# A shared expert's second products over all 128 rows of TensorE, with zeros in the matrix, in place of two products of 64 rows

## The chip, the cores and the metric

The kernel runs on one core of a Trainium2 chip. The metric is the time of one execution on the device, in microseconds. Before the change three runs took 928.37, 928.45 and 928.70 us; the median is 928.45.

## The reference

Eight sequences of 512 tokens with 128 features pass through three steps, each with a residual: an expert layer (weight 0.5), a mixing layer, and the same expert layer again. All matrices are float32. The expert layer has 64 routed experts and one shared expert, each with 64 hidden features. What it computes on a normalized token matrix `xf`:

```
shared = silu(xf @ Ws_up) @ Ws_down                     # (T,128)->(T,64)->(T,128)
cw     = weights of the 8 best of 64 experts per token, else 0
h      = silu(einsum('td,edf->etf', xf, W_up))          # all 64 experts
y      = einsum('etf,efd->etd', h, W_down)
out    = shared + einsum('etd,te->td', y, cw)
```

The change concerns the last product of `shared`, with `Ws_down` of 64 x 128.

## The kernel before

**Items and pairs.** An item is one sequence in one of the two expert layers, so there are 16 items of 512 tokens. Data is held transposed: features on the partitions, tokens along the free axis. Experts are taken two at a time, as two experts of 64 hidden features fill the 128 rows: 32 pairs for each item. For pair n, `up(n)` multiplies by `W_up` (`up_part`, L527) into an accumulator `ph` in PSUM and takes the silu on ScalarE into a tile `h` (L538). `scale(n)` multiplies `h` by the routing weights `cw` on VectorE (L544), which come by DMA from a scratch tensor. `down(n)` multiplies by `W_down` and adds into the item's accumulator `ys[i]`, 128 x 512 (L554).

**Order.** The order is written out by hand: one loop over n = 0 ... 32 x 16 + 14 does `up(n)`, the scaling of a pair some 20 steps back, and `down(n - 25)`. Engines work through their instructions in the order in which the program gives them, and on TensorE `up` and `down` products alternate. Between them generators insert the preparation of the next item (`prep`: normalization, the product for the router and the shared expert at L393, selection of experts), the mixing layer (L292, L299) and the residual (`finish`).

**The shared expert.** `prep(i)` computes the shared expert's hidden features, silu at L436, for one item at a time, 64 rows. Even items write rows 0 to 63 of a tile `hsh`; the following odd item writes rows 64 to 127 of the same tile. So `shared[i]` and `shared[i+1]` are one tile with two sequences in it.

**The place of the change.** When an even item i reaches pair 12 in `down` (`SHARED`), the accumulator of item i+1 is taken as well, and both items' second products are issued one behind the other at L567. The matrix tile `wsdn` holds `Ws_down` twice, in rows 0 to 63 and in rows 64 to 127. Item i's product takes the lower 64 rows of matrix and hidden tile and adds into `ys[i]`; item i+1's takes the upper 64 and starts `ys[i+1]`. The next products on TensorE are the ordinary `up` and `down` ones.

**Loading.** `wsdn` is loaded by two DMAs from `load_rest` (L160) on SP's queue, behind the first transfers of routing weights and ahead of the second half of `W_down`. On POOL the program begins with an identity matrix, a small constant and one memset of zeros into a part of `cent` (L139).

Of the kernel before, what the change touches and what calls it, by code (L numbers as in the profile page):

```python
# [8 lines left out]
F32 = mybir.dt.float32  # L9
# [4 lines left out]
P = 128  # L14
# [29 lines left out]
def macaron_kernel(  # L44
# [36 lines left out]
    nc = tc.nc  # L81
    B, T, D = x.shape
    E, _, F = w_up.shape
# [7 lines left out]
    const = ctx.enter_context(tc.tile_pool(name="const", bufs=1))  # L91
# [21 lines left out]
    def load_x(s, a=0, e=NT, queue=nc.sync):  # L113
        src = x[s].rearrange("(n p) d -> p n d", p=P)
        queue.dma_start(out=xs[s][:, a:e, :], in_=src[:, a:e, :])
# [2 lines left out]
    wdn = const.tile([P, NP, D], F32, name="wdn")  # L118

    wsl = const.tile([P, 2, 2, F], F32, name="wsl")  # L120
    wsdn = const.tile([P, D], F32, name="wsdn")
    cent = const.tile([P, D], F32, name="cent")
    bias_bc = const.tile([P, E], F32, name="bias_bc")
    wmix = const.tile([D, 2, D], F32, name="wmix")
# [8 lines left out]
    def load_down(e0, e1):  # L133
        nc.sync.dma_start(
            out=wdn[:, e0 // 2 : e1 // 2, :],
            in_=w_down[e0:e1].rearrange("(q two) f d -> (two f) q d", two=2),
        )

    nc.gpsimd.memset(cent[E:, :], 0.0)  # L139

    for n, (a, e) in enumerate(PIECES):
        load_x(0, a, e, (nc.sync, nc.scalar)[n % 2])
# [14 lines left out]
    def load_rest():  # L157

        for k in range(2):
            nc.sync.dma_start(out=wsdn[k * F : (k + 1) * F, :], in_=ws_down)  # L160
        load_down(E // 2, E)
        load_x(2)
        yield
        nc.sync.dma_start(out=wmix[:, 0, :], in_=wb)
        nc.sync.dma_start(out=wmix[:, 1, :], in_=wbf)
        yield
        nc.sync.dma_start(out=w12[:, 0, :], in_=w1[0].partition_broadcast(P))
        nc.sync.dma_start(out=w12[:, 1, :], in_=w2[0].partition_broadcast(P))
        nc.sync.dma_start(out=b_bc, in_=b.partition_broadcast(P))
        for s in range(3, B):  # L170
            yield
            load_x(s)
# [168 lines left out]
    shared = {}  # L341
# [159 lines left out]
    def finish(i, y, last=True):  # L501

        _, s = items[i]
        yield
        yt = norm.tile([P, NT, D], F32, tag="yt", name=f"yt{i}")
        y = y.rearrange("d (n p) -> d n p", p=P)
        yield from blocks(
            lambda f, q: yt[quad(q), :, quad(f)],
            lambda f, q: y[quad(f), :, quad(q)],
            D // B32,  # L510
            P // B32,
        )
        nc.vector.scalar_tensor_tensor(xs[s], yt, 0.5, xs[s], ALU.mult, ALU.add)
        if last:
            store(i, slice(0, NT))
# [34 lines left out]
    def down(n):  # L550
        i, pair = divmod(n, NP)
        if pair == 0 and i not in ys:
            ys[i] = ps_y.tile([P, T], F32, tag="y", name=f"y{i}")
        nc.tensor.matmul(  # L554
            ys[i],
            lhsT=wdn[:, pair, :],
            rhs=hs.pop(n),
            start=pair == 0 and i % 2 == 0,
            stop=pair == NP - 1 or n == total - ENDING - 1,
        )  # L560


        if i % 2 == 0 and pair == SHARED:
            ys[i + 1] = ps_y.tile([P, T], F32, tag="y", name=f"y{i + 1}")
            for k in range(2):
                rows = slice(k * F, (k + 1) * F)
                nc.tensor.matmul(  # L567
                    ys[i + k],
                    lhsT=wsdn[rows, :],
                    rhs=shared[i + k][rows, :],  # L570
                    start=k == 1,
                    stop=False,
                )
        if pair == NP - 1 and i + 1 < len(items):
            finishing.append(finish(i, ys.pop(i)))
# [33 lines left out]
    for n in range(total + DOWN_LAG - ENDING):  # L609
        i, pair = divmod(n, NP)  # L610
        if n < total:
            if i == 0 and pair == FIRST:
                run(coming)
                for g in range(CW_BUFS):
                    load_cw(g)
                loading = load_rest()
                next(loading)
            if i > 0 and pair == 0:
                while i not in shared:
                    next(coming)  # L620
            if i > 0 and pair == LAST_PREP:
                run(coming)
                coming = iter(())
            if i + 1 < len(items) and pair == FIRST_PREP[items[i + 1][0]]:
                coming = prep(i + 1)
            up(n)
# [5 lines left out]
        if n >= DOWN_LAG:  # L632
            down(n - DOWN_LAG)
            if finishing and next(finishing[0], finishing) is finishing:
                finishing.pop(0)
# [51 lines left out]
```

## Time and profile before

| | |
|---|---|
| median of three runs | 928.45 us |
| profiled execution | 928.27 us |
| its span, first to last instruction | 926.5 us |
| granted TensorE clock | 1.00 |
| matmul records at L527 / L554 / L567 | 1040 / 1004 / 32 |
| mean length of a record at L527, 512 columns | 593 ns |
| mean length of a record at L554 | 592 ns |
| mean length of a record at L567 | 641 ns |
| mean length of a weight load at L554 / L567 | 190 / 184 ns |
| DMA, mean rate over the span | 157 GB/s |

A float32 product is carried out in two passes, so it gives two matmul records and two weight loads. The records of matmuls overlap: a record of 592 ns says when a pass began and when its last result was written, and the next pass begins before that. How much of TensorE's time a pass takes is read from the distance between two starts. The profile calls TensorE's matmuls PE and its weight loads PEld; DVE is VectorE, ACT is ScalarE, POOL is GpSimd and SP issues DMAs. L567 means line 567 of the kernel. In a row of the timeline the columns are start and length in microseconds, engine, line, operation, tiles written and read, shapes, the number of instructions merged into the row, and in brackets the engine's idle time before it with what ended it.

### The profile page before, as it was taken

The numbers are of one execution on the slowest core, as the hardware profiler recorded it, in microseconds if no ns is written. First come the engines' busy times: TensorE is split into PE (matmuls) and PEld (weight loads), VectorE is DVE, ScalarE is ACT, GpSimd is POOL, SyncE is SP. The second block draws the span as 40 slices with busy tenths as digits, with TensorE's granted clock in tenths as the row PEclk, the third lists the DMA queues.
The fourth block names the chain that finished last, engine by engine and source line by source line (L and its number), as shares of the span: only waits on it lengthen the run. The fifth ranks groups of instructions, "written<-read, shape, count | busy, mean of one in ns | idle before, by whom it ended". The sixth has DMA issues, their size and how long they took to land.

```text
span 926.5 us, 8543 instructions
## 1 busy us (share of the span) xinstructions
PE 922.6 (100%) x2343; PEld 423.3 (46%) x2343; DVE 749.5 (81%) x2160; ACT 364.2 (39%) x600; POOL 39.8 (4%) x65
## 2 busy tenths in 40 slices
PE   9999999999999999999999999999999999999998
PEld 6444444444444444444444444444444444444445
DVE  6758978849497585969989899898998989989656
ACT  6533434334343343433434334343343433434330
POOL 1000000000000000000000000000000000000000
PEclk9999999999999999999999999999999999999999
DMA  7999986865949578566676756667576675766973
GB/s 179 228 202 204 215 183 143 187 135 134 192 110 193 112 159 164 139 140 135 143 160 138 161 133 157 156 150 164 130 163 151 151 162 128 160 156 151 190 150 84
DMA packets 88704, 145.72 MB, mean 157 GB/s; under 512 B 9616, under 2 KB 21584, under 8 KB 88656
## 3 DMA queue, kind: packets, MB, share of 16 engines
q1 hardware_dynamic: 88288, 145.05, 71.8%
q8 instruction: 18, 0.29, 0.2%
q14 instruction: 30, 0.25, 0.1%
q10 hardware_dynamic: 368, 0.13, 0.1%
HBM read 140.97 MB, written 4.19 MB: 157 GB/s over the span
## 4 chain that ended last, share of the span: by engine, by line
PE 100%; DVE 0%; issue 0%
PE ph L527 48%; PE y L554 47%; PE sl L393 2%; PE y L588 1%; PE y L567 1%; PE pfb L299 1%; PE pfb L292 1%; PE busy L181 0%; PE ps_ft L420 0%; DVE x L595 0%; PE cent_ps L187 0%; DVE zeros L176 0%
## 5 line engine op out<-in xcount | busy, mean ns | idle before, releaser
L527 PE MATMUL ph<-ut,wup 128*128 128x512 f32 (+2 forms) x1040 | 520.3, 586 | 0.0
L554 PE MATMUL y<-h,wdn 128*128 128x512 f32 x1004 | 510.2, 592 | 0.0
L538 ACT ACTIVATE h<-ph 128x512 f32<-128x512 f32 x512 | 300.5, 598 | 465.3 <-PE ph L527 455.0
L544 DVE TENSOR_TENSOR h<-h,cw 128x512 f32<-128x512 f32 x512 | 338.4, 686 | 36.0 <-DMA cw<-cw_t 29.7
L527 PEld LDWEIGHTS ph<-ut,wup 128*128 128x128 f32 x1040 | 194.7, 190 | 237.4 <-issue 231.8
L554 PEld LDWEIGHTS y<-h,wdn 128*128 128x128 f32 x1004 | 190.8, 190 | 240.1 <-issue 200.9
L248 DVE STREAM_TRANSPOSE yt<-y 32x128 f32<-32x128 f32 x256 | 79.9, 312 | 68.3 <-PE y L554 64.2
L248 DVE STREAM_TRANSPOSE ut<-u_f 32x128 f32<-32x128 f32 x240 | 72.2, 301 | 3.6
L248 DVE STREAM_TRANSPOSE aff<-sl 32x128 f32<-32x128 f32 x128 | 40.0, 312 | 4.1 <-PE sl L393 2.0
L248 DVE STREAM_TRANSPOSE mixt<-u_mix 32x128 f32<-32x128 f32 x128 | 38.7, 302 | 2.1
L248 DVE STREAM_TRANSPOSE cw_sb<-cwtok 32x128 f32<-32x128 f32 x128 | 38.4, 300 | 1.8
L228 DVE TENSOR_SCALAR u_f<-x,mv_f,rstd_f 128x128 f32<-128x128 f32 x64 | 18.0, 342 | 19.6 <-POOL rstd_f L224 19.6
L223 POOL TENSOR_SCALAR rstd_f<-mv_f 128x4 f32<-128x4 f32 x15 | 8.3, 552 | 502.9 <-DVE mv_f L222 502.9
L456 ACT ACT_TABLE_LOAD x15 | 19.2, 1283 | 23.4 <-DVE aff L248 23.4
L308 DVE SCALAR_TENSOR_TENSOR pfb<-u_mix,ident,pfb 128x129 f32<-128x129 f32 x16 | 5.7, 356 | 19.6 <-PE pfb L299 19.4
L538 ACT ACT_TABLE_LOAD x16 | 20.5, 1283 | 0.3
L224 POOL TENSOR_TENSOR rstd_f<-rstd_f,minus_half 128x4 f32<-128x4 f32 (+2 forms) x18 | 17.4, 966 | 4.1 <-DVE rstd_f L223 2.8
L228 DVE TENSOR_SCALAR u_mix<-x,mv_mix,rstd_mix 128x128 f32<-128x128 f32 x32 | 8.9, 343 | 9.9 <-POOL mixt L279 9.9
L393 PE MATMUL sl<-ut,wsl 128*128 128x512 f32 (+2 forms) x36 | 16.9, 550 | 0.0
L223 POOL TENSOR_SCALAR rstd_mix<-mv_mix 128x4 f32<-128x4 f32 x8 | 4.6, 576 | 280.0 <-DVE mv_mix L222 280.0
L436 ACT ACTIVATE hsh<-sl 64x512 f32<-64x512 f32 x16 | 9.5, 591 | 16.8 <-PE sl L393 16.8
L219 DVE BATCH_NORM_STATS2 st_f<-x 128x6 f32<-128x128 f32 x64 | 14.0, 277 | 1.9 <-DMA x<-in_L_attn_u_dram 1.8
(61 smaller groups left out, 247.8 us busy)
## 6 DMA issues: line engine op xcount, KB each, us to landing
cw<-cw_t SPq DMA_DIRECT2D x254, 512.0 KB, 6.7
cw_t<-cw_sb SPq DMA_DIRECT2D x16, 128.0 KB, 3.8
x<-in_L_attn_u_dram SPq DMA_DIRECT2D x7, 256.0 KB, 15.4
out_dram<-x SPq DMA_DIRECT2D x7, 256.0 KB, 3.1
wdn<-in_L_ffn_W_down_dram SPq DMA_DIRECT2D x2, 512.0 KB, 5.9
cw<-cw_t SPq DMA_DIRECT2D x4, 256.0 KB, 5.8
wup<-in_L_ffn_W_up_dram SPq DMA_DIRECT2D x4, 128.0 KB, 3.2
wup<-in_L_ffn_W_up_dram SPq DMA_DIRECT2D x1, 512.0 KB, 5.2
```

The source lines that it names most:

```text
L219: nc.vector.bn_stats(st[:, j, :], src[:, j, :])
L223: adds.tensor_scalar(rstd[:, a:e], mv[:, a:e, 1], EPS_LN, None, ALU.add)
L224: nc.gpsimd.tensor_tensor(rstd[:, a:e], rstd[:, a:e], minus_half[:, a:e], ALU.pow)
L228: nc.vector.tensor_scalar(u[:, j, :D], src[:, j, :], mv[:, j, 0:1], rstd[:, j : j + 1], ALU.subtract, ALU.mult,)
L248: nc.vector.transpose(dst(i, q), src(i, q))
L393: nc.tensor.matmul(sl[:, cols], lhsT=wsl[:, odd, :, :].rearrange("d a f -> d (a f)"), rhs=ut[:, cols], start=True, stop=True,)
L436: nc.scalar.activation(hsh[mine, :], sl[mine, :], AF.Silu)
L456: nc.scalar.activation(sig, aff, AF.Sigmoid)
L527: nc.tensor.matmul(ph[:, cols], lhsT=w, rhs=uts[i][:, cols], start=True, stop=True)
L538: nc.scalar.activation(h, ph, AF.Silu)
L544: nc.vector.tensor_tensor(h, h, cw_tiles[group][:, g, :], ALU.mult)
L554: nc.tensor.matmul(ys[i], lhsT=wdn[:, pair, :], rhs=hs.pop(n), start=pair == 0 and i % 2 == 0, stop=pair == NP - 1 or n == total - ENDING - 1,
```

## The change

The matrix tile becomes twice as wide, 128 x 2 x 128. Its first half holds `Ws_down` in rows 0 to 63 and zeros in rows 64 to 127; its second half holds zeros in rows 0 to 63 and `Ws_down` in rows 64 to 127. The zeros are written once, by two memsets on POOL. Both products then take all 128 rows of the matrix and all 128 rows of the hidden tile; the zeros cancel the other sequence's rows. Accumulators, start and stop flags, and the place in the order stay.

```diff
-    wsdn = const.tile([P, D], F32, name="wsdn")
+
+    wsdn = const.tile([P, 2, D], F32, name="wsdn")
...
     nc.gpsimd.memset(cent[E:, :], 0.0)
+    for k in range(2):
+        nc.gpsimd.memset(wsdn[(1 - k) * F : (2 - k) * F, k, :], 0.0)
...
         for k in range(2):
-            nc.sync.dma_start(out=wsdn[k * F : (k + 1) * F, :], in_=ws_down)
+            nc.sync.dma_start(out=wsdn[k * F : (k + 1) * F, k, :], in_=ws_down)
...
         if i % 2 == 0 and pair == SHARED:
             ys[i + 1] = ps_y.tile([P, T], F32, tag="y", name=f"y{i + 1}")
             for k in range(2):
-                rows = slice(k * F, (k + 1) * F)
                 nc.tensor.matmul(
                     ys[i + k],
-                    lhsT=wsdn[rows, :],
-                    rhs=shared[i + k][rows, :],
+                    lhsT=wsdn[:, k, :],
+                    rhs=shared[i + k],
                     start=k == 1,
                     stop=False,
                 )
```

## The prediction

> **What bounds the kernel.** I read the profile in this order: the busy shares, the chain of waits that ended last, the list of waits, and then the timeline of the one place that the change touches. The first three settle what the time is made of.
>
> ```profile
> PE 922.6 (100%) x2343; PEld 423.3 (46%) x2343; DVE 749.5 (81%) x2160; ACT 364.2 (39%) x600; POOL 39.8 (4%) x65
> ...
> PE 100%; DVE 0%; issue 0%
> PE ph L527 48%; PE y L554 47%; PE sl L393 2%; PE y L588 1%; PE y L567 1%; PE pfb L299 1%; PE pfb L292 1%; PE busy L181 0%; PE ps_ft L420 0%; DVE x L595 0%; PE cent_ps L187 0%; DVE zeros L176 0%
> ```
>
> The chain is TensorE from end to end. A busy TensorE alone would prove little, since its matmuls overlap, so the list of waits is needed too. Restricted to matmuls it has a single row:
>
> ```profile
> PE busy L181 <- DVE zeros L176: 1.0, 1, 1.0
> ```
>
> That is the first microsecond of the program. After it no matmul waits for another engine or for a transfer. What a stage costs is then the distance from one matmul's start to the next one's, and whatever is added to it is added to the end. Nothing later takes it back, since there is no later wait of TensorE to shorten.
>
> A product of float32 appears as two matmul records (two passes). Far from the change, passes start every 0.429 us: the last long stretch of the chain in order of time has 32 passes in 13.73 us.
>
> ```profile
> 900.96 13.73 PE y L554 x32
> ```
>
> **The place itself.** The changed products stand at L567, reached eight times (items 0, 2, ... 14), each time two products of two passes: 8 x 2 x 2 = 32 records. The timeline of TensorE around the first of them (start, length, engine, line, count):
>
> ```profile
> 50.73 1.02 PE L554 MATMUL y<-h,wdn 128*128 128x512 f32 x2
> 51.69 1.13 PE L567 MATMUL y<-hsh,wsdn 64*128 64x512 f32 x4
> 52.75 1.12 PE L527 MATMUL ph<-ut,wup 128*128 128x512 f32 x2
> 53.71 1.02 PE L554 MATMUL y<-h,wdn 128*128 128x512 f32 x2
> 54.57 1.02 PE L527 MATMUL ph<-ut,wup 128*128 128x512 f32 x2
> ```
>
> The reader is to look at the starts. The ordinary distance between two pairs of passes is 54.57 - 53.71 = 0.86 us. The four passes of L567 take 52.75 - 51.69 = 1.06 us where four at the ordinary rate take 1.72. So the two halves of the array do work at once: in the trace's starts, two passes begin within 0.01 us of each other, and the next two 0.53 us later. But the overlap isn't free. The pair before L567 occupies 51.69 - 50.73 = 0.96 us instead of 0.86, the pair after it again 53.71 - 52.75 = 0.96. The row of weight loads says why:
>
> ```profile
> 51.69 0.30 PEld L567 LDWEIGHTS y<-hsh,wsdn 64*128 64x128 f32 x4 [0.76 <-issue]
> ```
>
> Ordinary loads follow the previous one after an idle 0.24 us, while the pass before is still running. These start only after 0.76 us, together with their own passes: at the boundary the weights are not loaded ahead, and the array runs empty for about 0.10 us going in, and again coming out. The list of waits has that row eight times, 6.1 us in all, so 0.76 at every place.
>
> **The sum, part by part.** From 50.73 to 53.71 there are eight passes (two of L554, four of L567, two of L527) and they take 2.98 us. After the change all eight use all 128 rows. There are as many instructions as before, but none can share the array with another, so they run one after another with their weights loaded ahead: 8 x 0.429 = 3.43 us. The difference is 3.43 - 2.98 = +0.45 us (0.46 with the starts to the nanosecond), split so: four passes that lose their partner, 1.72 - 1.06 = +0.66; the two boundaries that go, 2 x 0.10 = -0.20. The stretch around the last of the eight places has the same starts (854.91, 855.86, 856.92, 857.88: 2.97 us), so I multiply by eight: **+3.65 us**, all of it on the path.
>
> _A rule against the trace._ The row: two passes on different halves start together, but each place costs 2.98 us in all. The Trainium skill, "TensorE: Matmul & The Clock Gate", Part 3, "Measured speedup vs the span model", says a group of tiles lasts as long as one matmul plus about 4 ns for each further tile. By that alone the present products would cost two passes of 0.429 at each place, and separating them would add 2 x 0.429 = 0.86 us, eight times 6.9 us. The trace agrees with the rule on the near-simultaneous starts, but the rule leaves out the slower starts around and inside the group, 4 x 0.10 us at each place. I take the row: +3.65, not +6.9. Both speak against this change; neither the rule nor the row offers a way to profit from it except the boundaries, and these are too small.
>
> **The other edits.** _Two memsets on POOL_, of 64x128 each. The nearest row is the one for `cent`, of the same size, and the row after it is what could be delayed:
>
> ```profile
> 1.41 0.20 POOL L139 MEMSET cent<- 64x128 f32 x1
> ...
> 3.68 1.10 POOL L224 TENSOR_TENSOR rstd_f<-rstd_f,minus_half 128x1 f32<-128x1 f32 x2 [2.08 <-DVE rstd_f L223]
> ```
>
> They are 2 x 0.20 = 0.40 us, put directly behind `cent` and ahead of POOL's first useful work, the power at L224, which waits 2.08 us for VectorE anyway. Cost nothing; without this cover they would delay the first normalization by up to 0.4 us. No DMA is issued from POOL there, and the issues of SP and ScalarE are not behind them. _The two loads of the matrix_ (SP, L160) keep size and count; the rows land at another stride. Issued at 28.4 and 29.5, landed at most 16.0 us later, so by 45.5, while the first use is at 51.69: 6.2 us to spare.
>
> _Waits that are added._ Each product now reads all 128 rows of the hidden tile, so item i's product needs item i+1's half too, and both need the zeros. Behind a waiting product stands everything on TensorE, its queue being the kernel's bound. But the second product needed that half already, and it is written long before:
>
> ```profile
> 34.63 0.59 ACT L436 ACTIVATE hsh<-sl 64x512 f32<-64x512 f32 x1 [1.12 <-PE sl L393]
> ```
>
> 35.2 against 51.69; at the last place 842.8 against 855.86. The zeros are set near 2 us. What handling further wait conditions costs TensorE itself is not in the trace as a row of its own. From below: nothing, as for the products of L554, which also wait for another engine's semaphore and still start every 0.43 us. From above: a pause like the ones at L567, 0.10 us at each place, 0.8 in all. A gain is excluded, since a wait can't start anything earlier. I take nothing, the nearer row.
>
> _Work behind._ VectorE, ScalarE and the DMA queue get 0.45 us more time per place. Their waits fall a little; none of them is on the chain.
>
> **Sum.** The profiled execution took 928.27 us, of which 926.5 are its span and 1.8 lie around it; with +3.65 it is 931.9. The median of the runs is 0.18 higher, 928.45, so I predict **932.1**.
>
> **Rivals.** _The pauses stay_ (10%). If the 0.10 us at the four starts came from something else than the 64-row form, such as the fresh accumulator of item i+1 or the switch between two operand sets, the eight full passes would keep them and cost 3.43 + 0.40 = 3.83 us: +0.85 a place, +6.8 in all, 935.3. Against it: ordinary products alternate accumulator, weights and operand at every pair and show no pause. In part, with one pause left at each place, it gives 932.9.
>
> _A new wait decides_ (3%). If the matrix landed over 6.2 us later than now, TensorE would stand at the first place; only there, since the matrix is loaded once. A landing twice as late (32 us) would give 61.5 - 51.7 = 9.8 us, 942. Against it: the same bytes in the same order.
>
> _Not slower_ (5%). The one mechanism: full-row passes without a mode change hand over faster than I assume, because two following products stream the same hidden tile. To come out even, the four passes would have to take 1.72 - 0.45 = 1.27 us, 0.32 each; only then is the removal of the boundaries worth what the sharing was. At 0.32, the time is 928.5. Against it: no pass of 512 columns in the trace starts less than about 0.43 us after another on the same rows, whatever it reads.
>
> _It doesn't do what it says_: if the present two products had not overlapped, the change would only remove pauses. The 1.06 us for four passes exclude that.
>
> **How the numbers follow.** The likeliest case has 82%, with a range of its own from 931.7 to 932.9 (rounding of the starts and scatter of the runs below; one pause left at each place above). The range on record, 931.2 to 933.4, adds part of the first rival; its full form and the other two stay outside. A difference of 0.2%, 1.9 us, is about what a measurement of this kernel can tell from no change. The likeliest case and the first two rivals are slower by more than that; the third divides between no change (3%) and faster (2%).
>
> **What would show it.** In the changed profile: L567 as 32 records of 128*128, starting 0.43 us apart; no 0.76 us of idle before their weight loads, 0.24 instead; the stretch from L554's first pass to the next L554 3.43 us at all eight places; TensorE still with no wait after the first microsecond, and span and TensorE's busy time both longer by 3.6 to 3.7 us. Pauses that remain, a stop at the first place, or starts closer than 0.43 us would make the prediction wrong.

## The result and the profile after

The changed kernel took 932.61 us (median of four runs, 932.24 to 933.18) against 928.55 before. The ratio is 1.0040 with a 95% interval of 1.0028 to 1.0051: slower, with the whole interval above 1. The time lies inside the range, 0.5 us above the forecast. The profiled execution is the slowest of the four, 933.18, with a span of 931.4.

The timeline of TensorE around the first place, after the change (line numbers from L530 to L568 stand for L527 to L567 before):

```profile
50.59 1.02 PE L557 MATMUL y<-h,wdn 128*128 128x512 f32 x2
51.45 1.88 PE L568 MATMUL y<-hsh,wsdn 128*128 128x512 f32 x4
53.17 1.02 PE L530 MATMUL ph<-ut,wup 128*128 128x512 f32 x2
54.03 1.02 PE L557 MATMUL y<-h,wdn 128*128 128x512 f32 x2
```

The four passes take 53.17 - 51.45 = 1.72 us, and the distances ahead of them and behind are 0.86 each. From L557 to L557 it is 3.44 us where it was 2.98. In the starts to the nanosecond every one of the eight places shows the same: six passes from the second of L557 to the second of L530 in 2.575 us, where it was 2.115. That is +0.46 each and +3.68 in all, so the forecast's term is there in full. The weight loads show the same: each follows after the ordinary idle time of 0.24 us instead of 0.76.

```profile
51.02 0.19 PEld L568 LDWEIGHTS y<-hsh,wsdn 128*128 128x128 f32 x1 [0.24 <-issue]
51.45 0.19 PEld L568 LDWEIGHTS y<-hsh,wsdn 128*128 128x128 f32 x1 [0.24 <-issue]
```

But the span grew by 4.9, not by 3.7. The page and the waits of TensorE's matmuls show the rest:

```profile
PE 926.2 (99%) x2343; PEld 427.2 (46%) x2343; DVE 749.6 (80%) x2160; ACT 364.0 (39%) x600; POOL 40.1 (4%) x67
...
PE 96%; DVE 2%; ACT 0%; issue 0%; DMA 0%; POOL 0%; ACTq 0%; POOLq 0%
```

```profile
PE busy L184 <- DVE zeros L179: 1.0, 1, 1.0
PE ph L530 <- ACT h L541: 1.0, 1, 1.0
```

TensorE's busy time grew by 926.2 - 922.6 = 3.6 us, as it should, but there is one wait more, and 4% of the chain runs through other engines. That is no 4% of lost time: for some 25 us the chain follows VectorE and ScalarE while TensorE still works, and only the wait at its end is lost. The timeline has this stop of TensorE near 103 us, TensorE first, then ScalarE:

```profile
102.95 1.02 PE L557 MATMUL y<-h,wdn 128*128 128x512 f32 x2
104.99 1.13 PE L530 MATMUL ph<-ut,wup 128*128 128x512 f32 x2 [1.02 <-ACT h L541]
```

```profile
96.28 0.60 ACT L541 ACTIVATE h<-ph 128x512 f32<-128x512 f32 x1 [1.12 <-PE ph L530]
101.32 1.28 ACT L459 ACT_TABLE_LOAD   x1 [4.44 <-DVE aff L251]
102.61 0.42 ACT L459 ACTIVATE rsig<-aff 128x256 f32<-128x256 f32 x1
103.05 1.28 ACT L541 ACT_TABLE_LOAD   x1
104.34 2.56 ACT L541 ACTIVATE h<-ph 128x512 f32<-128x512 f32 x5
```

ScalarE stands 4.44 us in front of the router's sigmoid (L459), whose input, the transposed logits, VectorE delivers late. The silus queued behind it, which empty TensorE's accumulators, wait with it, and TensorE's pair is due at 102.95 + 0.86 = 103.81 but starts at 104.99: 1.18 us, and 0.10 more at the next pair. In the kernel before the same chain ran, earlier (ScalarE, then the TensorE pair that was due there):

```profile
98.37 1.28 ACT L456 ACT_TABLE_LOAD   x1 [1.81 <-DVE aff L248]
99.66 0.42 ACT L456 ACTIVATE rsig<-aff 128x256 f32<-128x256 f32 x1
100.10 1.28 ACT L538 ACT_TABLE_LOAD   x1
101.39 2.07 ACT L538 ACTIVATE h<-ph 128x512 f32<-128x512 f32 x4
103.49 1.02 PE L527 MATMUL ph<-ut,wup 128*128 128x512 f32 x2
```

ScalarE's sequence is 101.32 - 98.37 = 2.95 us later after the change, while TensorE's own place there is 103.81 - 103.49 = 0.32 later. So the kernel before had 2.95 - 0.32 - 1.18 = 1.45 us to spare here, in an execution whose list of waits shows nothing.

VectorE's lateness is there some 20 us earlier already. The same scaling of a hidden tile, before the change and after it:

```profile
77.68 0.69 DVE L544 TENSOR_TENSOR h<-h,cw 128x512 f32<-128x512 f32 x1 [2.45 <-DMA cw<-cw_t]
```

```profile
80.62 0.69 DVE L547 TENSOR_TENSOR h<-h,cw 128x512 f32<-128x512 f32 x1 [3.67 <-ACT h L541]
```

This is the first pair of the second item. It starts 2.94 us later, and from there VectorE works without a pause up to the logits. The row after the change names a silu, but the silu of this pair was done at 43.5 us. The trace's landings tell more: the last part of the transfer that the row waits for landed at 77.55 us before and at 80.49 after, 0.12 us ahead of the row both times. So both waits ended with routing weights, and these came later. Is this stop the change's doing, or could it have met either kernel? That, and how the 2.98 us of the old place are composed, is what the experiments ask.

### The profile page after: what moved, and what is told of

The parts are those of the page before. It is cut to its first block, busy times and chain, and to the rows that moved or that the text cites. A ratio compares the mean times of both kernels' runs of the same rounds, so it can differ in the third digit from the quotient of the medians.

```text
span 931.4 us, 8547 instructions
## 1 busy us (share of the span) xinstructions
PE 926.2 (99%) x2343; PEld 427.2 (46%) x2343; DVE 749.6 (80%) x2160; ACT 364.0 (39%) x600; POOL 40.1 (4%) x67
## 4 chain that ended last, share of the span: by engine, by line
PE 96%; DVE 2%; ACT 0%; issue 0%; DMA 0%; POOL 0%; ACTq 0%; POOLq 0%
PE ph L530 46%; PE y L557 45%; PE y L568 1%; PE sl L396 1%; PE y L589 1%; PE pfb L302 1%; PE pfb L295 1%; DVE h L547 1%; DVE yt L251 1%; DVE ut L251 1%; DVE aff L251 0%; DMA x<-in_L_attn_u_dram 0%; ACT L541 0%; ACT L459 0%; ACT h L541 0%
## 5 line engine op out<-in xcount | busy, mean ns | idle before, releaser
L530 PE MATMUL ph<-ut,wup 128*128 128x512 f32 (+2 forms) x1040 | 519.6, 586 | 1.0 <-ACT h L541 1.0
L557 PE MATMUL y<-h,wdn 128*128 128x512 f32 x1004 | 510.2, 592 | 0.0
L530 PEld LDWEIGHTS ph<-ut,wup 128*128 128x128 f32 x1040 | 195.3, 190 | 236.5 <-issue 229.4
L557 PEld LDWEIGHTS y<-h,wdn 128*128 128x128 f32 x1004 | 190.8, 190 | 240.1 <-issue 201.6
L227 POOL TENSOR_TENSOR rstd_f<-rstd_f,minus_half 128x4 f32<-128x4 f32 (+2 forms) x18 | 17.3, 964 | 3.7 <-DVE rstd_f L226 2.4
L396 PE MATMUL sl<-ut,wsl 128*128 128x512 f32 (+2 forms) x36 | 16.9, 550 | 0.1
```

What stands on the lines that cost most here:

```text
L227: nc.gpsimd.tensor_tensor(rstd[:, a:e], rstd[:, a:e], minus_half[:, a:e], ALU.pow)
L396: nc.tensor.matmul(sl[:, cols], lhsT=wsl[:, odd, :, :].rearrange("d a f -> d (a f)"), rhs=ut[:, cols], start=True, stop=True,)
L530: nc.tensor.matmul(ph[:, cols], lhsT=w, rhs=uts[i][:, cols], start=True, stop=True)
L557: nc.tensor.matmul(ys[i], lhsT=wdn[:, pair, :], rhs=hs.pop(n), start=pair == 0 and i % 2 == 0, stop=pair == NP - 1 or n == total - ENDING - 1,
```

## The experiments

**The changed kernel again**, with no edit.

> The changed kernel once more, with nothing edited. Theory 1 (only the passes cost): span 930.2 us if TensorE waits for nothing behind the first microsecond, and the one stop of 1.2 us near 103 us in the first profile is a matter of that execution; the runs then lie between 932.0 and 933.3, the lower end being 928.4 + 3.66. Rival (the stop belongs to the change): every profile has a stop of about 1.2 us near 103 us, and no run is under 932.9.

Five runs, 931.92 to 932.63, median 932.18; the kernel before in the same series 928.53 (ratio 1.0036, interval 1.0023 to 1.0050). The difference of the medians is 3.65, that of the fastest runs 931.92 - 928.26 = 3.66. The profile has no stop, so the stop doesn't come with every execution of the changed kernel; the scaling that began at 80.62 in the first profile begins at 77.52 here. Its span is 930.8 and not 930.2: the first place begins 0.66 us later, a matter of the program's first 8 us, called the head from here on (last section). The kernel before was run 33 times in this series and reached from 928.26 to 931.13, six times above 929.0. So its own time scatters upwards too.

**The other edits without the products**: wide matrix, zeros, and loads stay, the products take 64 rows again.

```diff
             for k in range(2):
+                rows = slice(k * F, (k + 1) * F)
                 nc.tensor.matmul(
                     ys[i + k],
-                    lhsT=wsdn[:, k, :],
-                    rhs=shared[i + k],
+                    lhsT=wsdn[rows, k, :],
+                    rhs=shared[i + k][rows, :],
```

> The wide matrix with its zeros, the two memsets and the loads at the new stride stay, the products take 64 rows each again. Theory 1 (only the passes cost, the other edits nothing): 928.5, with L569's passes in two groups as in the kernel before. Rival (layout, memsets or loads delay the early transfers and bring the stop near 103 us): 929.0 to 929.7, with a stop of TensorE there.

928.53 in 13 runs, as before; ratio 1.0000, interval 0.9992 to 1.0008. Its timeline has the old place back:

```profile
51.35 1.02 PE L557 MATMUL y<-h,wdn 128*128 128x512 f32 x2
52.30 1.13 PE L569 MATMUL y<-hsh,wsdn 64*128 64x512 f32 x4
53.36 1.12 PE L530 MATMUL ph<-ut,wup 128*128 128x512 f32 x2
54.32 1.02 PE L557 MATMUL y<-h,wdn 128*128 128x512 f32 x2
```

54.32 - 51.35 = 2.97 us. Memsets, layout and loads cost nothing that the interval, some 0.8 us to either side, would show; the cost lies in the rows of the products.

**The two 64-row products apart**, one pair of the loop between them.

```diff
-        if i % 2 == 0 and pair == SHARED:
-            ys[i + 1] = ps_y.tile([P, T], F32, tag="y", name=f"y{i + 1}")
-            for k in range(2):
...
+        if i % 2 == 0 and pair in (SHARED, SHARED + 1):
+            k = pair - SHARED
+            if k == 1:
+                ys[i + 1] = ps_y.tile([P, T], F32, tag="y", name=f"y{i + 1}")
...
```

> The kernel before with the upper product one ordinary pair later, so that each 64-row product stands alone between full-row ones. Nothing is shared any more and the boundaries are doubled. Theory (the overlap gains, each boundary of 64 and 128 rows costs 0.10 us): four passes at 0.43 and four boundaries at 0.10 for each place, 3.83 us where the kernel before takes 2.98: +0.85 x 8 = +6.8, 935.3. Rival (a product of 64 rows costs a boundary nothing, only sharing counts): +0.45 x 8, 932.1, as the changed kernel.

938.62 (938.20 to 938.95, four runs; ratio 1.0106, interval 1.0091 to 1.0121), 3.3 us above the theory's figure. The direction is the theory's, its price for a boundary, that is a change between passes of 128 and of 64 rows, is not:

```profile
50.72 1.02 PE L554 MATMUL y<-h,wdn 128*128 128x512 f32 x2
51.67 1.12 PE L568 MATMUL y<-hsh,wsdn 64*128 64x512 f32 x2
52.72 1.13 PE L527 MATMUL ph<-ut,wup 128*128 128x512 f32 x2
53.69 1.02 PE L554 MATMUL y<-h,wdn 128*128 128x512 f32 x2
54.64 1.12 PE L568 MATMUL y<-hsh,wsdn 64*128 64x512 f32 x2
```

Six passes from 50.72 to 53.69 take 2.97 us where six ordinary ones take 2.57: one product alone costs 0.40 us in pauses, for one boundary going in and one coming out. So a boundary is 0.20, not 0.10. In the starts to the nanosecond, two handovers from pass to pass are slow at each: 523 and 533 ns going in, 519 and 533 coming out, instead of 429. The pass ahead of the boundary hands over late, and so does the first pass behind it.

**Both products on the same 64 rows**, so that no two passes can share the array, but with only two boundaries at a place.

```diff
-                rows = slice(k * F, (k + 1) * F)
+                rows = slice(0, F)
```

> The kernel before with both products on the lower 64 rows of matrix and hidden tile (item i+1 gets item i's hidden features, so its output is another). Nothing can be shared, there is one boundary going in and one coming out. Theory (a pause belongs to a change between 64 and 128 rows): 8 passes at 0.43 and two pauses of 0.10 in each place, 3.63 us, +0.65 x 8 = +5.2, 933.7. Rival (a pause belongs to every pass of 64 rows, since its weights are not loaded ahead): four or five pauses, 3.83 to 3.93, 935.3 to 936.1.

935.11 (935.07 to 935.42, four runs; ratio 1.0070, interval 1.0053 to 1.0086). The time is the rival's, but the trace decides against its mechanism. Matmuls first, then weight loads:

```profile
50.62 1.02 PE L554 MATMUL y<-h,wdn 128*128 128x512 f32 x2
51.57 1.98 PE L567 MATMUL y<-hsh,wsdn 64*128 64x512 f32 x4
53.48 1.12 PE L527 MATMUL ph<-ut,wup 128*128 128x512 f32 x2
54.45 1.02 PE L554 MATMUL y<-h,wdn 128*128 128x512 f32 x2
```

```profile
51.57 0.29 PEld L567 LDWEIGHTS y<-hsh,wsdn 64*128 64x128 f32 x2 [0.76 <-issue]
52.11 0.19 PEld L567 LDWEIGHTS y<-hsh,wsdn 64*128 64x128 f32 x1 [0.24 <-issue]
52.54 0.19 PEld L567 LDWEIGHTS y<-hsh,wsdn 64*128 64x128 f32 x1 [0.24 <-issue]
53.48 0.30 PEld L527 LDWEIGHTS ph<-ut,wup 128*128 128x128 f32 x2 [0.76 <-issue]
```

Between the boundaries the loads of 64 rows do run ahead of their passes, with the ordinary 0.24 us of idle, and the passes follow at 429 ns. Only at the change of the row count does the load wait, 0.76 us, and start together with its own pass. Eight passes take 54.45 - 50.62 = 3.83 us, so 3.43 and 0.40 for the two boundaries. The Trainium skill, "TensorEngine Tiling (Array Packing)", "Key Properties", says that changing the tiling mode drains TensorE while changing only the tile does not. The loads agree: they wait at a change of the row count and nowhere else, and the price is 0.20 us a change here. That the array is empty in between can't be read from the records, whose ends are modelled.

With this the three arrangements of 64-row products and the change add up from two terms: sharing is worth 2 x 0.429 = 0.86 us at each place, two boundaries cost 0.40 (0.391 in the starts of half_same_rows).

| kernel | halves share time | boundaries at a place | per place against before | x 8 | span minus 926.5 |
|---|---|---|---|---|---|
| before | yes | 2 | 0 | 0 | 0 |
| changed (full_again) | no | 0 | 0.86 - 0.40 | 3.7 | 4.3, of it 0.66 in the head |
| same rows | no | 2 | 0.86 | 6.9 | 6.8 |
| apart | no | 4 | 0.86 + 0.40 | 10.1 | 9.9 |

**What makes the stop.** The first idea was the load of sequence 2, which stands ahead of routing weights on SP's queue. It was moved behind them in both kernels.

```diff
         load_down(E // 2, E)
+        yield
         load_x(2)
         yield
```

> The changed kernel with the load of sequence 2 moved behind the first routing weights that follow it. Theory (the stop near 103 us comes from routing weights that land late while the DMA engines are full until 54 us, VectorE falls behind, ScalarE's sigmoid at L460 waits for it and holds the silu): no stop, span 930.2, time 932.1 and less scatter. Rival (the stop has another origin): as full_again, 932.2 to 933.2, with a stop near 103 us in the profile.

> The kernel before with the load of sequence 2 moved as in full_x2_later. Theory: the kernel before has no stop to remove in most runs, so 928.4, the best that these edits give; ratio to before between 0.9995 and 1.0. Rival (some runs of before have the stop too): up to 0.3 us better in the median.

932.48 (932.05 to 932.90) and 928.86 (928.17 to 929.90), ratio of the second to before 1.0003, interval 0.9994 to 1.0011. Neither is better nor scatters less. The second one's profile shows a stop at another time, with the same form (ScalarE, then TensorE):

```profile
157.06 1.28 ACT L457 ACT_TABLE_LOAD   x1 [4.72 <-DVE aff L249]
...
160.08 2.06 ACT L539 ACTIVATE h<-ph 128x512 f32<-128x512 f32 x4
160.73 1.12 PE L528 MATMUL ph<-ut,wup 128*128 128x512 f32 x2 [1.30 <-ACT h L539]
```

The products there have 64 rows: the stop needs no part of the change. Near 98 us this execution is as early as the kernel before; it is late one item further on, where VectorE waits 4.4 us for routing weights between 118 and 140 us and the kernel before not at all. So the load's place is not the cure.

**More early transfers in the kernel before**: 512 KB that nobody reads, ahead of the load of sequence 2.

```diff
+    spare = const.tile([P, 2, NT, D], F32, name="spare")
...
         load_down(E // 2, E)
+        for k in range(2):
+            nc.sync.dma_start(
+                out=spare[:, k], in_=x[2].rearrange("(n p) d -> p n d", p=P)
+            )
         load_x(2)
```

> The kernel before with 512 KB of transfers more ahead of the load of sequence 2, into a tile that nobody reads. At about 200 GB/s these delay the routing weights by some 2.5 us; the slack of ScalarE's silu near 102 us in the profile of before is about 1.5 us. Theory (the stop is a property of the early transfers, not of the change): TensorE stops near 103 us, 0.5 to 2 us, time 929 to 930.5. Rival (the stop belongs to the change): 928.5, no stop.

The median rose to 930.02 in 21 runs, from 928.47 to 931.64; ratio 1.0014, interval 1.0007 to 1.0020. Its profile fell on the shortest of these executions (928.47) and has no stop, so where the longer ones lose their time was not seen in this kernel; only that more early transfers make them frequent.

**The sigmoid later on ScalarE.** If ScalarE's order is the link, it helps to issue the sigmoid only behind VectorE's match_replace, where item 0 has it already.

```diff
-        if i > 0:
-            nc.scalar.activation(sig, aff, AF.Sigmoid)
...
         if i == 0:

             hidden()
-            nc.scalar.activation(sig, aff, AF.Sigmoid)
+        nc.scalar.activation(sig, aff, AF.Sigmoid)
```

> The kernel before with 512 KB of early transfers more (half_more_dma, whose runs reach from 928.5 to 931.6 with a median of 930.0) and the later sigmoid. Theory (the stops come from the sigmoid's place): the median falls to 928.5 to 928.9. Rival: it stays at 929.5 or above.

> The changed kernel with the router's sigmoid issued on ScalarE behind VectorE's match_replace, two steps of the loop later, so that it no longer waits in ScalarE's queue for a late transpose of the logits. Theory (the stops near 103 and 159 us come from this order in ScalarE's queue): no stop in the profile, runs between 931.9 and 932.7 with the head's scatter alone, median 932.1. Rival (VectorE's lateness reaches TensorE through the scaled hidden tiles anyway): runs up to 933.2 as before.

> The kernel before with the later sigmoid alone. Theory: the runs of before that reach 929 to 931 go, the fastest stay, median 928.4 against 928.5, ratio 0.9995 to 1.0. Rival: the sigmoid so late holds VectorE, which then delays the routing weights: 929 or more.

With the extra transfers the median fell from 930.02 to 928.64 (13 runs, highest 929.48). The two belong to different series; against before in the same series the second is 0.9994, interval 0.9986 to 1.0002, which doesn't overlap the 1.0007 to 1.0020 without the edit. Its profile shows a VectorE that is late and a TensorE that is not (VectorE, ScalarE, and two pairs of TensorE from the timeline):

```profile
80.01 0.69 DVE L547 TENSOR_TENSOR h<-h,cw 128x512 f32<-128x512 f32 x1 [2.93 <-DMA cw<-cw_t]
...
100.71 1.28 ACT L471 ACT_TABLE_LOAD   x1 [0.76 <-DVE aff L253]
...
101.73 1.02 PE L530 MATMUL ph<-ut,wup 128*128 128x512 f32 x2
103.45 1.02 PE L530 MATMUL ph<-ut,wup 128*128 128x512 f32 x2
```

The scaling waits for routing weights and starts 80.01 - 77.68 = 2.33 us later than before, and the logits let ScalarE go on 100.71 - 98.37 = 2.34 us later, while TensorE's place is the same, 103.45 against 103.49. With 1.45 us to spare the old order would have cost about 0.9 us here (an estimate from these rows); with the new one ScalarE does two silus more ahead of the sigmoid, and TensorE's list of waits has nothing after the first microsecond. So it is through this order that the early transfers reach TensorE's time. The changed kernel took 932.22 (931.87 to 932.84; the profiled one, 932.84, has no stop but a late head), the kernel before 928.45 (13 runs, 928.12 to 929.39) while the unedited one in that series had 928.96 (25 runs, 928.26 to 932.65). The interval of the last against before, 0.9986 to 1.0002, includes 1: it is the best version seen, mainly by scattering less upwards (the fastest runs are 928.12 and 928.26), but its gain isn't settled.

## Why the prediction was right, point by point

- **The bound.** Right for executions without a stop. Spans follow TensorE's pass starts to 0.2 us once the head is taken out. Where it went too far is "Nothing later takes it back" together with "Their waits fall a little; none of them is on the chain": both were read from one execution's list of waits, which shows no slack. With 1.45 us to spare near 103 us, an execution whose routing weights come 2.9 us later has a stop there; why they come later in one execution than in another stays open. It is 1.28 of the profiled execution's 4.9 us. What share it has in the 0.5 us between forecast and median is open, since the other three executions left no trace; the second series, at 932.18, lies 0.1 from the forecast. Of the signs named beforehand, TensorE's busy time (+3.6) came, while "no wait after the first microsecond" and a span longer by 3.6 to 3.7 did not come in this execution. The range held the stop by luck: its upper part was meant for pauses that stay.
- **The sum.** +3.65 predicted, +3.68 in the starts, +3.65 between the medians of the second series; in the first these differ by 4.06. Right, because it was taken as the whole stretch, boundary to boundary.
- **Its split.** "four passes that lose their partner" for +0.66 and "the two boundaries" for -0.20 was wrong: sharing is worth +0.86 and the boundaries -0.40. The pause inside the group of four, 0.53 instead of 0.43, belongs to the boundaries too. The prediction's paragraph on the rule counts four slow starts of 0.10, which is the right sum; the split has two of them. The error cancels in the change but not in half_apart, whose expectation missed by 3.3 us because of it.
- **The rule against the row.** That it "leaves out the slower starts" holds: by the span model alone the cost would have been 6.9, and it was 3.7.
- **The other edits at nothing.** Right: wide_half_rows is 1.0000 of before. In the changed kernel's profile the two memsets end at 2.0 us, and the power at L227 still waits 1.69 us for VectorE.
- **Added waits.** Right at nothing: the passes of L568 start every 0.429 us.
- **The rivals.** The pauses did not stay; no new wait stands at L568; a full-row pass of 512 columns never started sooner than 0.429 us after another.

## What to carry to other kernels

On this TensorE two products of 64 rows on different halves of the array really share their time, but each switch between 64 and 128 rows costs 0.20 us: float32 products of 512 columns gained 0.86 and paid 0.40, and if sharing fails, the same pair loses 0.40. Other sizes and types were not measured here. Price an edit by the whole stretch between two undisturbed starts; a split by eye inside it can be wrong while the sum is right. A list of waits without a wait doesn't say how near one is: look for the engine whose queue holds a late instruction in front of what the bound needs, and give that instruction a later place.

## What the hardware showed beyond that

The first 8 us differ from one execution to the next. In full_again the first passes of L396 took 0.80 us for two, against 0.49 in the kernel before, and the next two started at 7.50 instead of 6.84:

```profile
5.50 0.80 PE L396 MATMUL sl<-ut,wsl 128*128 128x128 f32 x2
...
7.50 0.39 PE L396 MATMUL sl<-ut,wsl 128*128 128x128 f32 x2
```

The trace's record of the granted clock begins with full speed at 6.9 us here and at 5.4 us in the kernel before; over the twelve profiles it lies between 4.2 and 7.3. It came late, 6.3 or more, in four of the five profiles with the two memsets and in none of the other seven. Their times speak against a link: 8 of 13 runs of wide_half_rows, which has the memsets, are at 928.56 or below, as are 18 of 33 of the kernel before. Whether anything of the memsets reaches the head was not tested more closely than that.
